# The order of work in the second step of a two-step graph layer, changed in four of seven parts

## The chip, the core and the metric

The kernel runs on one core of a Trainium2 chip. The metric is device time in microseconds (us): the median of several executions. A profile is one more execution, recorded by the hardware profiler. Engines are named as in the profile: PE (matrix products and transposes), DVE (vector), ACT (scalar functions), POOL (GpSimd, which also issues the indirect gathers) and SP (which issues the other transfers). PEld is PE's loading of weights, which overlaps its products.

## The reference

The input is x (3327 x 256) and a sparse weighted adjacency matrix adj (3327 x 3327, about four entries in a row beside the diagonal). After a layer norm and a relu, two steps of the same kind follow, and a last layer norm is added to x:

```python
R = S + jnp.eye(N, dtype=X.dtype)
R = R / R.sum(-1, keepdims=True)
for n in range(STEPS):                       # 2
    A = _top_p_attention(Xa, W1, W2, W3)     # softmax(q k^T), cut to the top 0.9 of its mass, row sums 1
    Xf = R @ Xf
    Xa = A @ Xa
    Z = Z + Xf @ U1[n].T + Xa @ U2[n].T
h = X + Z
```

The costly part is A: 3327 logits in each of 3327 rows, their exponentials, the smallest set of the largest ones that holds 0.9 of each row's sum, and the product of what is left with Xa.

## The kernel before

**Tiles.** A row tile is 128 rows of the matrix ("row i" below is such a tile), and there are 26. One row of exponentials is a tile e of 128 x 3328 in SBUF; it stays there while its threshold is found and is cut in place.

**Two steps, 26 slots each, seven parts in a slot.** The program is written out by Python generators. Each generator is one piece of work on one row, and yields where another may come in between. In slot i of a step, one letter stands for each of them, and the table PLAN (L1001) says in which of the seven parts each is advanced by one stage. The letters of the second step:

- m: `measured_twice` (L635) of row i+1. Its first stage turns the row's sum into a guess (ACT L586 to L591 and L641, POOL L642 to L646). Stage 2 is a pass of ACT over the row (L599, function Relu) and stage 3 a second pass (Sign); stage 4 works out a second guess (DVE L653 and L654, ACT L655 to L657, POOL L658 to L660), stage 5 is a third pass (Sign), stage 6 works out the exponent of a correction (DVE L665 and L666, ACT L668 to L671, POOL L673 to L678).
- n: the rest of m of the slot before, for row i. Its stage 7 is one ACT instruction (L680) that reads what POOL's L678 wrote; stage 8 is DVE L682 to L685 and gives the threshold's guess.
- d: `settle` (L693) of row i, all on DVE: a pass over the row that copies what lies below the guess (L699), twice ten MAX8 (L704), then six rounds of MAX8 and MATCH_REPLACE8 (L711, L713) in two stages, which give the exact threshold (L718 to L723).
- c: the rest of d of the slot before: the pass over the row that cuts it at the threshold (DVE L726), then L727 to L730.
- w: `weights` (L551) of row i+2: one stage is one of four pieces of logits, two products on PE (L566) into a PSUM buffer of two banks (pool ps_l, two buffers) and an exponential on ACT (L570; the last piece L574 and L576).
- q: the first two stages of `weights` of row i+3, which are those of `project` (L517): first the products for queries and law (PE L525, L527) and their copies to SBUF (ACT L530 and L534), then DVE L540 on the copy mq and six POOL instructions on ms (L543 to L548).
- s: `spread` of row i (PE L868, then DVE L984), the sparse product with R. g: `refetch` of row i+2 (five indirect gathers on POOL, L860). f: `finish` of row i-2 (DVE L891, L459, L460; POOL L466, L467; DVE L898; POOL L899 to L901; the transfer out).

Around the letters, each part begins with four transposes of a row on PE (L771) and their copy on ACT (L773), two parts ahead of use, and ends with a piece of the row sum: four products of 128 x 256 (L785) that add up in the one buffer pa. A row's sum starts in part 5 of the slot in which the row is cut and ends in part 4 of the next slot; there ACT scales it into SBUF (L792), and then the next row's sum may start in pa.

**What sets the order.** PE, ACT and DVE run in the order in which the text writes the instructions: at the end, every instruction of these three is tied to the one before it on its engine (L1067 to L1070). POOL and SP are not tied; their order is chosen when the program is built, by when inputs are ready in the builder's own estimate, and is fixed from then on. Waits between engines are on semaphores.

The loop over the parts:

```python
for k in range(PARTS):
    ...
    if summing:
        sums.turn(g, min(i, NT - 1))
    for c in "bb" + PLAN[step][k]:
        next(work[c], None)
    if summing:
        ended = sums.sum(g)
```

Of the kernel before, what the change touches and what calls it, by code (L numbers as in the profile page):

```python
# [342 lines left out]
def guess_graph_layer(ctx, tc, x, adj, w1t, w2t, w3t, u1t, u2t, ln_g, ln_b, out, flag):  # L343
# [646 lines left out]
    def refetch(t):  # L990
# [8 lines left out]


    PLAN = (("mdsssa", "mdsssa", "edawwp", "sda", "mpdea", "mdgawwq", "emdgq"),  # L1001
            ("cmss", "cnms", "wwnfd", "mdsss", "smwqdfg", "mqdfg", "mwdf"))
    LATE = (1, 4)
    trace, begin = nc.cur_bb.bb.instructions, len(nc.cur_bb.bb.instructions)
    work = dict(m=none, d=none, f=none)
# [71 lines left out]
@with_exitstack  # L1077
def tile_graph_layer(ctx, tc, *args):
    keep = ctx.enter_context(tc.tile_pool(name="keep", bufs=1))
    flag = keep.tile([1, 1], I32, tag="flag", name="flag")  # L1080
    guess_graph_layer(tc, *args, flag)
    failed = tc.nc.values_load(flag[0:1, 0:1], min_val=0, max_val=1 << 20)
    with tc.If(failed > 0):
        search_graph_layer(tc, *args)
# [34 lines left out]
```

## Time and profile before

| what | value |
|---|---|
| median of 3 runs | 1568.15 us (1564.48 to 1574.11) |
| the profiled execution, its own time | 1572.46 us |
| its span, first to last instruction | 1570.7 us |
| granted TensorE clock, mean | 0.944 |
| second step, from its first pieces to the end | about 899 to 1571 us of the span |
| row sums' copies (L792) of the second step | first at 980.24, last at 1552.69 |
| between two of them, most rows | 23.53 to 23.56 us |
| two longer slots | 25.48 and 24.59 us |
| the last four | 20.60, 22.01, 19.54 and 13.59 us |

How to read the lines that follow. A line of a timeline has the start in us from the span's start, the duration, the engine, the line of the kernel, the operation, what it writes and reads with shapes, and in square brackets the idle time of that engine just before it and what released it. An idle time is shown only where it is over a few tenths. In a view by windows, each engine has its busy time and in brackets its count of instructions. A stalled instruction counts as busy: POOL's time includes what it stands still for.

### The profile page before, as it was taken

To read this page: it belongs to the slowest core of one execution; us is meant where nothing else is said; L and a number is where in the kernel's file an instruction comes from. 1 tells how busy PE (TensorE), PEld (TensorE's weight loads), DVE (VectorE), ACT (ScalarE), POOL (GpSimd) and SP (SyncE) were. 2 spreads that over 40 slices of the span, in tenths; PEclk is the share of its full clock that TensorE was granted. 3 is DMA by queue.
4 is the path that set the end of the run, shared out by engine and by line. 5 is a ranking of instruction groups with operands and counts; after the bars stand their busy time and mean duration, and the time that the engine had idled before them with its cause. 6 is when DMAs were issued, how large, how long until landed. Compare 5 with 4: busy or idle time off the path is not lost.

```text
span 1570.7 us, 22630 instructions
## 1 busy us (share of the span) xinstructions
PE 1331.4 (85%) x6495; PEld 997.6 (64%) x6495; DVE 1227.8 (78%) x3824; ACT 1104.2 (70%) x2476; POOL 1004.7 (64%) x1491
## 2 busy tenths in 40 slices
PE   5857888988988989889898937998998999899884
PEld 3523666766666767667676725776776767767674
DVE  4457788878987878787786248989988889889892
ACT  5527566757766677677674378898898898898941
POOL 6313464564755656655565156888888888888842
PEclk9978998999999999999999968999999999999997
DMA  7554343443533543444423121122122122122200
GB/s 218 167 163 128 107 128 103 117 129 104 142 114 99 150 111 113 137 115 111 125 63 89 58 72 51 56 77 71 56 76 67 55 81 63 58 81 64 58 18 20
DMA packets 97687, 149.81 MB, mean 95 GB/s; under 512 B 15985, under 2 KB 60528, under 8 KB 97552
## 3 DMA queue, kind: packets, MB, share of 16 engines
q1 hardware_dynamic: 78400, 104.00, 21.7%
q0 software_dynamic: 16640, 42.69, 10.7%
q10 hardware_dynamic: 2512, 1.57, 0.3%
q8 instruction: 54, 0.88, 0.2%
q14 instruction: 81, 0.66, 0.2%
HBM read 120.93 MB, written 27.28 MB: 94 GB/s over the span
## 4 chain that ended last, share of the span: by engine, by line
PE 35%; POOL 22%; ACT 19%; DVE 10%; issue 7%; DMA 4%; another core or an unknown queue 1%; SPq 0%; ACTq 0%; POOLq 0%; DVEq 0%
PE pa L785 17%; ACT ja L599 9%; POOL xg L860 7%; PE pt L771 5%; POOL g L677 4%; PE pr L868 4%; PE pl L566 4%; DMA at<-in_adj 3%; ACT e L570 3%; ACT eT L773 2%; PE pz L881 2%; DVE e L726 2%; DVE cand L704 1%; POOL rstd L467 1%; DVE fm L803 1%
## 5 line engine op out<-in xcount | busy, mean ns | idle before, releaser
L773 ACT COPY eT<-pt 128x512 f32<-128x512 f32 (+1 forms) x364 | 201.3, 554 | 238.4 <-PE pt L771 168.4
L785 PE MATMUL pa<-xw,eT 128*128 128x256 f32 x1352 | 334.9, 390 | 29.3 <-ACT xa L792 28.5
L785 PE MATMUL pa<-x,eT 128*128 128x256 f32 x1352 | 351.4, 404 | 4.1 <-ACT eT L773 2.4
L851 POOL DMA_INDIRECT ac<-in_adj,index x130 | 179.8, 1383 | 247.0 <-DVE mq L540 160.7
L599 ACT ACTIVATE ja<-e,g 128x3328 uint8<-128x3328 f32 x106 | 325.7, 3073 | 0.1
L785 PEld LDWEIGHTS pa<-xw,eT 128*128 128x128 f32 x1352 | 252.6, 193 | 93.0 <-ACT xa L792 33.7
L785 PEld LDWEIGHTS pa<-x,eT 128*128 128x128 f32 x1352 | 261.3, 201 | 58.7 <-issue 16.3
L704 DVE MAX8 cand<-w 128x8 f32<-128x168 f32 (+1 forms) x1040 | 251.3, 317 | 0.0
L771 PE MATMUL pt<-ident,e 128*128 128x128 f32 x1144 | 181.8, 280 | 38.7 <-DVE e L726 35.4
L771 PEld LDWEIGHTS pt<-ident,e 128*128 128x128 f32 x1144 | 145.0, 145 | 77.7 <-issue 32.3
L860 POOL DMA_INDIRECT xg<-bx,index x130 | 163.2, 1255 | 48.2 <-issue 34.9
L566 PE MATMUL pl<-k,qT 64*128 64x416 f32 x832 | 187.8, 556 | 4.7 <-ACT qT L530 4.2
L699 DVE SCALAR_TENSOR_TENSOR w<-e,g 128x3328 f32<-128x3328 f32 x44 | 163.9, 3725 | 0.7
L860 POOL DMA_INDIRECT xg<-vx,index x130 | 134.0, 1031 | 43.9 <-issue 35.0
L726 DVE SCALAR_TENSOR_TENSOR e<-e,rec 128x3328 f32<-128x3328 f32 x44 | 162.0, 3681 | 0.1
L868 PE MATMUL pr<-xg,ac 128*128 128x257 f32 (+1 forms) x520 | 137.7, 387 | 23.4 <-DVE s L984 20.0
L803 DVE TENSOR_REDUCE fm<-at 128x4 f32<-128x512 f32 (+1 forms) x182 | 115.8, 638 | 52.1 <-DMA at<-in_adj 50.4
L570 ACT ACTIVATE e<-pl 128x832 f32<-128x832 f32 x132 | 113.2, 866 | 7.6 <-PE pl L566 6.8
L868 PEld LDWEIGHTS pr<-xg,ac 128*128 128x128 f32 x520 | 90.0, 193 | 33.9 <-DVE s L984 20.3
L566 PEld LDWEIGHTS pl<-k,qT 64*128 64x128 f32 x832 | 71.4, 190 | 51.3 <-issue 42.7
L711 DVE MAX8 bb<-cand 128x8 f32<-128x160 f32 x286 | 92.7, 324 | 6.4
L884 DVE TENSOR_TENSOR sv<-pz,x 128x256 f32<-128x256 f32 x26 | 11.0, 423 | 97.3 <-ACT xw L882 89.9
(221 smaller groups left out, 2211.6 us busy)
## 6 DMA issues: line engine op xcount, KB each, us to landing
at<-in_adj SPq DMA_DIRECT2D x156, 256.0 KB
cx<-ac SPq DMA_DIRECT2D x26, 384.0 KB
ac<-cx SPq DMA_DIRECT2D x26, 384.0 KB
bx<-e SPq DMA_DIRECT2D x26, 128.5 KB
own<-bx SPq DMA_DIRECT2D x26, 128.5 KB
x<-in_x SPq DMA_DIRECT2D x13, 256.0 KB
xr<-in_x SPq DMA_DIRECT2D x26, 128.0 KB
ax<-e SPq DMA_DIRECT2D x26, 128.0 KB
```

What stands on the lines that cost most here:

```text
L566: PE.matmul(pl[:, a, :wd], qT[p, :], keys[step][p].rearrange("p a b -> p (a b)")[:, c : c + wd], start=True, stop=True)
L570: S.activation(e.rearrange("p (a n) -> p a n", a=2)[:, :, c : c + wd], pl[:, :, :wd], AF.Exp, accum_out=za[:, n : n + 1])
L599: S.activation(ja, e, f, bias=guess, scale=sign, accum_out=total)
L699: V.scalar_tensor_tensor(w, e, col(16), e, ALU.is_lt, ALU.mult, accum_out=d2)
L704: V.max(cand[:, 8 * s : 8 * s + 8], w[:, s * SEG : min(NP, (s + 1) * SEG)])
L726: V.scalar_tensor_tensor(e, e, at(1), e, ALU.is_ge, ALU.mult, accum_out=ra)
L771: PE.transpose(pt[:, j, :], e[:, (j0 + j) * P : (j0 + j + 1) * P], ident)
L773: S.copy(eT[:, :w, :], pt[:, :w, :])
L785: PE.matmul(self.pa, eT[:, c - 4 * k, :], self.xa[:, j, :], start=c == 0, stop=c == NT - 1)
L851: G.indirect_dma_start(out=ac[:, k, :], out_offset=None, in_=rows, in_offset=bass.IndirectOffsetOnAxis(ap=index[:, t, k : k + 1], axis=0), ...
L860: G.indirect_dma_start(out=xg[:, k, :w], out_offset=None, in_=rows, in_offset=bass.IndirectOffsetOnAxis(ap=index[:, t, k : k + 1], axis=0))
L868: PE.matmul(pr[:, :w], ac[:, k, :], own if k == KT - 1 else xg[:, k, :w], start=k == 0, stop=k == KT - 1)
```

## The change

One line of the table PLAN, that of the second step, is written anew. The first step, the stages themselves and all other code stay.

```diff
     PLAN = (("mdsssa", "mdsssa", "edawwp", "sda", "mpdea", "mdgawwq", "emdgq"),
-            ("cmss", "cnms", "wwnfd", "mdsss", "smwqdfg", "mqdfg", "mwdf"))
+            ("cmss", "cnms", "nmfd", "dwwsss", "smdfg", "mqdfgwwq", "mdf"))
     LATE = (1, 4)
```

Read part by part, in the second step:

- Part 3: the two pieces of logits (ww) leave its start. The second ACT pass over a row (m, stage 3) comes here from part 4, behind n and ahead of f and d.
- Part 4: the first two pieces of logits come here, behind d and ahead of the last three s. m is gone.
- Part 5: the third piece of logits (w) and the first stage of the projection (q) leave it.
- Part 6: the order is now m (the third ACT pass), q (first stage), d, f, g, two pieces of logits (third and fourth), q (second stage, with DVE L540 and POOL L543 to L548). Before, it was m, q (second stage), d, f, g.
- Part 7: the fourth piece of logits leaves it.

In each slot the same stages run for the same rows as before: m still advances six times, w four times, q twice.

## Prediction

> **What bounds the kernel now.** I read the page first, then the timelines of the second step (from 899 us on), one engine at a time, then the chain of waits there. The diff leaves the first step alone, so only the second counts. The page shows four busy engines and no plain bound:
>
> ```profile
> PE 1331.4 (85%) x6495; PEld 997.6 (64%) x6495; DVE 1227.8 (78%) x3824; ACT 1104.2 (70%) x2476; POOL 1004.7 (64%) x1491
> ```
>
> In the second step the row sum's copy (L792) returns every 23.53 to 23.56 us for most rows: that is the slot. One such slot in the view by windows (busy us by engine, PE, PEld, DVE, ACT, POOL):
>
> ```profile
> 1158.90:1182.50 23.60, 21.42 (x113) 16.58 (x111) 21.22 (x67) 20.82 (x43) 20.70 (x31) 1.00 0.22 68
> ```
>
> All four have 20.7 us or more, so the end is set by how they hand over. POOL's timeline in this slot, start and duration first:
>
> ```profile
> 1177.52 0.57 POOL L676 TENSOR_TENSOR g<-g,half 128x1 f32<-128x1 f32 x1
> 1178.19 3.82 POOL L677 TENSOR_SCALAR g<-g 128x1 f32<-128x1 f32 x1
> 1182.12 0.31 POOL L678 TENSOR_SCALAR g<-g 128x1 f32<-128x1 f32 x1
> ...
> 1183.89 3.56 POOL L643 TENSOR_SCALAR g<-g 128x1 f32<-128x1 f32 x1
> ```
>
> L677 and L643 work on 128x1 and take 0.30 and 0.19 us in other slots. They stand still under DVE's two passes over a row:
>
> ```profile
> 1171.78 0.21 DVE L540 SCALAR_TENSOR_TENSOR mq<-mq 128x64 f32<-128x64 f32 x1
> ...
> 1174.63 0.27 DVE L665 TENSOR_SCALAR g<-oa,g 128x1 f32<-128x1 f32 x1 [0.30 <-ACT ja L599]
> ...
> 1178.25 3.68 DVE L726 SCALAR_TENSOR_TENSOR x<-x,rec 128x3328 f32<-128x3328 f32 x1
> ```
>
> POOL's queue has no wait for another engine in this slot: 23.54 us = 16.63 of its own (20.70 less the two stalls, plus gaps of about 0.1 between instructions and 0.3 between gathers) + stalls of 3.52 and 3.37. ACT does wait, for POOL:
>
> ```profile
> 1158.92 0.29 ACT L680 ACTIVATE g<-g 128x1 f32<-128x1 f32 x1 [2.18 <-POOL g L678]
> ...
> 1167.86 0.48 ACT L792 ACTIVATE xa<-pa,ra 128x256 f32<-128x256 f32 x1
> ...
> 1170.70 0.28 ACT L534 COPY mq<-pq 128x130 f32<-128x130 f32 x1
> 1170.86 0.60 ACT L773 COPY eT<-pt 128x512 f32<-128x512 f32 x1
> 1171.34 3.09 ACT L599 ACTIVATE ja<-x,g 128x3328 uint8<-128x3328 f32 x1
> ```
>
> From here on times count from the start of L680 (1158.92). The loop that closes a slot: L680 0; L792 8.94; third ACT pass 12.42 to 15.46; L665 15.71; L726 19.33 to 23.01; L677 released; L678; next L680 23.54.
>
> [...] here two gathers under these passes took 4.22 and 4.40 us where 0.95 is usual, at 944.99 and 949.71. So neither kind of POOL work hides under a pass. [...] the pass behind L680 needs nothing from POOL and waits 2.18 us with it.
>
> **The change part by part.** No instruction is added or removed; four things move within a slot.
>
> 1. *The second ACT pass to the third part, the first two logits pieces behind it.* On ACT the order from 0 is pass, copy, two pieces (1.69), copy, pass (3.08), L792. It becomes pass, copy, pass, copy, two pieces, L792. The same five things stand ahead of L792: it starts at 8.94 again. That no 3 us pass stands directly before it buys nothing, since ACT has no gap there. PE reaches the row sum's end about 1.6 us earlier (its logits come later) but the next row's sum needs the single pa buffer: its wait for L792 grows from 1.31 to about 3 us. On DVE, L653's wait of 1.22 for the second pass goes: the pass now ends at 6.8, DVE is there at 7.9. DVE is 1.2 ahead until part 6. Value on the closing loop: nothing, because L655 still queues behind L792 and the copy (9.76).
>
> 2. *Third piece and projection leave part 5.* On ACT 0.85 + 0.30 us less lie between L657 and the copy eT ahead of the third pass. But that copy waits for PE: L792 ends 9.42, the sum's eight instructions 1.83, transposes 0.60, so 11.9; in the kernel before it started at 11.94. The third pass stays at 12.42. Value: nothing; ACT idles 1.1 us there instead.
>
> 3. *Projection copies (L530, L534) behind the third pass.* Now L534 is done at 15.46 + 0.15 + 0.28 = 15.89. L540 on DVE needs it, and the written order puts L540 after the rounds of the sixth part and *before* L665. DVE is there at 14.1 (the rounds ended at 15.4 before; less the 1.22 of part 1 and L540's own place) and waits 1.8. L540 at 15.92, L665 at 16.16 where it was 15.71: **+0.45**. Queued behind: L666, the last three rounds, L898, L726 (19.33 -> 19.78). POOL's six instructions on ms (L543 to L548, 2.30 us from L543's start to L673's) also wait for L540: they began at 15.08, straight after L467, and now begin at 16.24 (L540 + 0.32, as at 938.66 and 938.98).
>
> 4. *What is late next.* POOL then has ms 2.30 and L673 to L678: 18.54, 19.03, 19.42, 19.76 for L676. DVE's L726 starts at 19.78. An instruction that starts 0.06 to 0.08 before a pass is stalled too (L677 above, L673 at 1201.83). So L676 is caught rather than L677. The pass ends at 23.46; L676 needs 0.4 more (a 0.73 us L900 ended 0.5 after such a pass), L677 and L678 0.8: 24.65, L680 at once. The new slot is 24.65, **+1.11** = 0.45 for L726 and 0.66 for one more instruction behind it. If L676 slips through, L726 waits 0.6 and L677 is caught: 24.55. POOL no longer fills its queue: it has 1.1 us idle before L543, inside a longer slot.
>
> The moved pieces (third and fourth, now behind L534 on ACT; L668 at 18.05 instead of 16.26) are covered: ACT would reach the next L680 at 22.2 and waits for POOL until 24.65. Without that cover the 1.1 us of part 2 would count. PE is done with its slot at 23.2 and has its wait for L792 as reserve. Gathers on POOL (five of 1.25) keep their place; SP's queue gets no new wait.
>
> Sum, against the profiled execution's own 1572.5 (span 1570.7 plus 1.8 around it). 21 slots have the loop whole: 21 x 1.11 = +23.3. At the step's start L678 ended before L726 began, at 944.34 and 968.05, and L680 followed within 1 to 2.5 us; with L540 late both are caught. The next L680s move from 944.96 and 970.39 to about 949.4 and 975.5: +5. One gather waited 2.1 us at 1189, and that slot and the next were 3.0 longer in all; POOL's new slack takes some 2 of it: -2. The first slot puts ten gathers ahead of L660 (L665 waits 8.24): a different order on POOL there could give 0 to 4, taken as -1. The last four rows have no projection, and L653 waits for nothing in them: 0. Sum **+25**: 1597 on that execution's scale, which is 4.3 above the median of the runs shown; on the median **1593**.
>
> **Unknown costs.** POOL's order is not the written one (L466 and L467 stand ahead of L543 though written after), so the new one is not certain: ms first is what its readiness asks for, since L540 precedes L665 on DVE. Interleaved, L678 is still last of twelve. Per slot: 0.7 (L677 caught) to 1.4 (L675 caught), so +12 to +32 with the start between 0 and +6.
>
> **Rivals.**
> - *POOL stays the bound, no change.* If L673 to L678 run ahead of the ms group, L678 ends at 16.5 + 2.6 = 19.1, before L726; then the closing loop is short and POOL's 16.63 + 6.9 sets the slot: 23.54, 1564 to 1574. For it: POOL never waits today. Against: L673 becomes ready 0.5 us after L543.
> - *Faster.* DVE's lost waits (1.22 + 0.30) come through and the slot falls to 22.7, the shortest at the step's start: 21 x 0.84 = -18, 1550. This needs L678 done before L726 *and* POOL's passes overlapping idle time; it decides at a POOL demand under 22.7, and POOL's own 16.63 + 6.9 is 23.5 wherever a pass falls. Nearly excluded.
> - *Worse.* Gathers come to stand behind L658 and L659 (ready 10.9), so that ms and all of L673 to L678 fall under the pass: L678 near 26, 21 x 2 = +42, 1610. Against: the gathers' buffer is free at 5.3, long before.
>
> **How the numbers follow.** Loop over L540: 0.72, own range 1578 to 1604. No change 0.15. Worse 0.09. Faster 0.04. About 1% (15.7 us) is what a measurement of this kernel can tell from no change. Slower by more: 0.72 less 0.04 for its low end, plus 0.09 = 0.77. Within: 0.15 + 0.04 = 0.19. Faster 0.04. The range takes in most of the no-change case and the bounds of the stall: 1570 to 1606.
>
> **What would show it.** Right: slots of 24.3 to 25 in the second step; DVE waiting 1.5 to 2 us at L540 for L534; POOL waiting about 1 us at L543 for L540; L676 or L677 at 3.5 us or more; PE's wait for L792 near 3; no wait at L653. Wrong: L673 ahead of L543 on POOL, slots of 23.5, or a third pass that starts before 12.

## The result, and the profile after

The changed kernel takes 1644.37 us (median of 4 runs, 1640.33 to 1645.67), the kernel before 1567.33 on the same chip: 1.048 of it, interval 1.044 to 1.052. The prediction was 1593, with a range of 1570 to 1606. It had the sign, and 25 of the 77 us.

The profiled execution of the new kernel took 1640.33 us, 67.9 more than that of before. (The medians are 77 apart, as the one profiled before was 5 us above its median and the one after 4 below.) From the copies L792 in ACT's timeline, the 67.9 come together as follows:

| where | before | after | difference |
|---|---|---|---|
| first L792 of the second step, from the span's start | 980.24 | 985.21 | +5.0 |
| the 21 slots after it | 496.71 (mean 23.65) | 559.11 (mean 26.62) | +62.4 |
| from there to the end of the span | 93.8 | 94.3 | +0.5 |

In the first part of the page, after, only PE has more work to show, though it executes the same 6495 instructions:

```profile
PE 1366.5 (83%) x6495; PEld 1029.9 (63%) x6495; DVE 1227.8 (75%) x3824; ACT 1104.9 (67%) x2476; POOL 1006.9 (61%) x1491
```

They took 35.1 us longer. The new slots run from 24.96 to 27.17 us. The view by windows, after, for one of the shortest and one of the longest (slot, busy time of PE, PEld, DVE, ACT and POOL, granted clock, DMA share, GB/s):

```profile
1027.70:1052.66 24.96, 21.15 (x112) 16.70 (x111) 21.11 (x64) 20.80 (x42) 20.92 (x31) 1.00 0.22 64
1293.22:1320.39 27.17, 23.64 (x112) 18.76 (x111) 21.11 (x65) 20.80 (x43) 20.89 (x31) 0.87 0.20 59
```

DVE, ACT and POOL have the same work in both. PE's 112 instructions take 2.49 us more in the second, and its mean granted clock there is 0.87. PE's timeline, after, shows which instructions: the eight products that start a row sum, once L792 has emptied pa.

```profile
1037.17 1.99 PE L785 MATMUL pa<-xw,eT 128*128 128x256 f32 x8 [3.71 <-ACT xa L792]
...
1302.69 3.78 PE L785 MATMUL pa<-xw,eT 128*128 128x256 f32 x8 [3.53 <-ACT xa L792]
...
1309.83 1.99 PE L785 MATMUL pa<-xw,eT 128*128 128x256 f32 x8
```

The wait for L792 was 1.3 us; now it is over 3. In two of the 21 slots the eight products behind it still take 1.99 us, in nine 2.67 to 3.45, and in ten 3.78, about half their rate. A few us later (1309.83) they are at full rate again. What is late next is in ACT's timeline, after, in the same slot; times from L680 (1293.22) are 8.94 for L792, 14.14 for the copy eT and 14.62 for the third pass, which was at 12.42:

```profile
1293.22 0.29 ACT L680 ACTIVATE g<-g 128x1 f32<-128x1 f32 x1 [2.70 <-POOL g L678]
...
1302.16 0.48 ACT L792 ACTIVATE xa<-pa,ra 128x256 f32<-128x256 f32 x1
...
1307.36 0.59 ACT L773 COPY eT<-pt 128x512 f32<-128x512 f32 x1 [3.25 <-issue]
1307.84 3.07 ACT L599 ACTIVATE ja<-e,g 128x3328 uint8<-128x3328 f32 x1
```

ACT's 3.25 us are called "issue", but the copy follows the products and transposes on PE (the transposes L771 start at 1306.26 and take 1.06, so they end at 1307.32); in the 24.96 us slot the same wait is 1.04 us and is put down to PE's L771. DVE's timeline, after:

```profile
1311.36 0.23 DVE L540 SCALAR_TENSOR_TENSOR mq<-mq 128x64 f32<-128x64 f32 x1 [4.22 <-ACT mq L534]
...
1311.52 0.27 DVE L665 TENSOR_SCALAR g<-oa,g 128x1 f32<-128x1 f32 x1
1315.13 3.68 DVE L726 SCALAR_TENSOR_TENSOR e<-e,rec 128x3328 f32<-128x3328 f32 x1
```

And POOL's, after:

```profile
1311.71 0.34 POOL L543 TENSOR_SCALAR ms<-mq,ms 128x1 f32<-128x1 f32 x1 [3.49 <-DVE mq L540]
...
1314.93 3.92 POOL L675 TENSOR_SCALAR g<-g 128x1 f32<-128x1 f32 x1
...
1320.05 0.31 POOL L678 TENSOR_SCALAR g<-g 128x1 f32<-128x1 f32 x1
```

L726 catches L675, so that three instructions (L676 to L678) follow the pass where one did; then L680 starts the next slot. The table of waits, after, for 1275 to 1492 us puts the same chain together (us in total, times, longest):

```profile
PE pa L785 <- ACT xa L792: 31.6, 9, 3.7
DVE mq L540 <- ACT mq L534: 31.4, 8, 4.2
POOL ms L543 <- DVE mq L540: 25.4, 8, 3.5
ACT g L680 <- POOL g L678: 21.3, 8, 2.7
```

In the kernel before (1155 to 1395 us) the first of these was 13.3 us in 9 waits, and the wait of ACT for L678 was the same 21.3, in 9.

The slot with the full clock, 24.96 us (two of the 21 are so), is what the prediction's working should be held against. There L540 starts at 15.94 after L680 (predicted 15.92), L543 at 16.29 (16.24), L726 at 19.71 (19.78). So the 62.4 us split, with no experiment yet, into 21 x (24.96 - 23.65) = 27.5 for the predicted loop and 21 x (26.62 - 24.96) = 34.9 for PE's clock. The second is close to the 35.1 us that PE's busy time grew by.

### The profile page after: what moved, and what is told of

The parts are those of the page before. It is cut to its first block, busy times and chain, and to the rows that moved or that the text cites. A ratio compares the mean times of both kernels' runs of the same rounds, so it can differ in the third digit from the quotient of the medians.

```text
span 1638.6 us, 22607 instructions
## 1 busy us (share of the span) xinstructions
PE 1366.5 (83%) x6495; PEld 1029.9 (63%) x6495; DVE 1227.8 (75%) x3824; ACT 1104.9 (67%) x2476; POOL 1006.9 (61%) x1491
## 4 chain that ended last, share of the span: by engine, by line
PE 34%; ACT 31%; POOL 14%; DVE 7%; issue 7%; DMA 4%; another core or an unknown queue 2%; SPq 0%; ACTq 0%; POOLq 0%; DVEq 0%
ACT ja L599 16%; PE pa L785 16%; POOL g L675 5%; PE pt L771 4%; PE pr L868 4%; ACT eT L773 4%; DMA at<-in_adj 3%; PE pl L566 3%; ACT e L570 3%; PE pz L881 3%; POOL g L676 1%; PE pz L930 1%; PE pk L486 1%; ACT e L574 1%
## 5 line engine op out<-in xcount | busy, mean ns | idle before, releaser
L785 PE MATMUL pa<-xw,eT 128*128 128x256 f32 x1352 | 359.7, 412 | 78.7 <-ACT xa L792 78.5
L785 PEld LDWEIGHTS pa<-xw,eT 128*128 128x128 f32 x1352 | 268.1, 205 | 135.1 <-ACT xa L792 84.6
L771 PE MATMUL pt<-ident,e 128*128 128x128 f32 x1144 | 186.9, 286 | 26.9 <-DVE e L726 12.3
L566 PE MATMUL pl<-k,qT 64*128 64x416 f32 x832 | 192.1, 553 | 5.9 <-ACT qT L530 5.4
L771 PEld LDWEIGHTS pt<-ident,e 128*128 128x128 f32 x1144 | 150.2, 148 | 65.7 <-issue 18.2
L860 POOL DMA_INDIRECT xg<-bx,index x130 | 157.7, 1213 | 51.3 <-issue 33.2
L699 DVE SCALAR_TENSOR_TENSOR w<-e,g 128x3328 f32<-128x3328 f32 x44 | 164.3, 3733 | 0.7
L726 DVE SCALAR_TENSOR_TENSOR e<-e,rec 128x3328 f32<-128x3328 f32 x44 | 162.1, 3683 | 0.1
L868 PE MATMUL pr<-xg,ac 128*128 128x257 f32 (+1 forms) x520 | 141.7, 395 | 23.2 <-DVE s L984 20.2
L570 ACT ACTIVATE e<-pl 128x832 f32<-128x832 f32 x132 | 114.0, 872 | 8.4 <-PE pl L566 6.5
L566 PEld LDWEIGHTS pl<-k,qT 64*128 64x128 f32 x832 | 85.5, 198 | 49.2 <-issue 36.9
L675 POOL TENSOR_SCALAR g<-g 128x1 f32<-128x1 f32 x26 | 83.7, 3218 | 2.5
```

The lines of the kernel that those rows point to most:

```text
L566: PE.matmul(pl[:, a, :wd], qT[p, :], keys[step][p].rearrange("p a b -> p (a b)")[:, c : c + wd], start=True, stop=True)
L570: S.activation(e.rearrange("p (a n) -> p a n", a=2)[:, :, c : c + wd], pl[:, :, :wd], AF.Exp, accum_out=za[:, n : n + 1])
L675: G.tensor_scalar(col(12), col(12), col(12), 1.0e-12, ALU.mult, ALU.add)
L699: V.scalar_tensor_tensor(w, e, col(16), e, ALU.is_lt, ALU.mult, accum_out=d2)
L771: PE.transpose(pt[:, j, :], e[:, (j0 + j) * P : (j0 + j + 1) * P], ident)
L785: PE.matmul(self.pa, eT[:, c - 4 * k, :], self.xa[:, j, :], start=c == 0, stop=c == NT - 1)
```

## The experiments

Two theories at the start. **Clock:** the longer idle time costs PE its full rate, and the rest is the predicted loop over L540 and POOL. **Order:** POOL's and DVE's order alone makes the longer slot, and PE's longer products hide behind it.

The kernels ran on several chips, on which the kernel before took 1580.02 us (experiments 1 to 4), 1492.16 (8 to 11), 1494.37 (5, 6 and 12) and 1491.87 (7). They differ in the clock granted in the first step: from 300 to 700 us it was 0.95 to 0.97 in the kernel before, and 1.00 in experiment 10. So each ratio is against the kernel before on the same chip; the changed kernel itself ran on the first chip alone. "Slot" is the mean of 21 slots of the second step from L792 to L792 in the one profiled execution (23.65 before, 26.62 after), and a slot's "sum" is the eight products behind the L792 that opens it.

**1. The projection back in part 5, only the second pass moved (third and fourth pieces stay behind f and g).**

```diff
-            ("cmss", "cnms", "nmfd", "dwwsss", "smdfg", "mqdfgwwq", "mdf"))
+            ("cmss", "cnms", "nmfd", "dwwsss", "smqdfg", "mqdfgww", "mdf"))
```

> The changed kernel with only the projection put back: its first stage in part 5 and its second in part 6, both ahead of the rounds, as before the change; the logits stay in two pairs and the second pass in part 3. Theory A (late L540 delays L665 and POOL's ms group, and PE's long wait for L792 sends its clock down): L540 waits for nothing, POOL's ms group follows L467 at once, slots of 23.5 us where PE's first eight products after L792 take 2.0 us, and up to 24.4 where they take 3.8 (then ACT's 21.1 us of work and 3.3 us of idle time make the slot): 1566 to 1592 us. Theory B (the second pass in part 3, or the new order of the gathers on POOL, is what costs): the projection makes little difference, over 1615 us.

Measured: 1.0058 (1.0035 to 1.0081), slot 24.10. Slots of 24.6 to 25.3 us (26.6 once) and of 23.3 to 24.1 take turns, but for four in a row of 23.5. PE's timeline of this kernel, and then POOL's, a short slot (from 1080.76) and a long one (from 1104.26):

```profile
1081.30 3.54 PE L785 MATMUL pa<-xw,eT 128*128 128x256 f32 x8 [1.35 <-ACT xa L792]
...
1104.80 1.99 PE L785 MATMUL pa<-xw,eT 128*128 128x256 f32 x8 [0.31 <-ACT xa L792]
```

```profile
1092.12 0.33 POOL L678 TENSOR_SCALAR g<-g 128x1 f32<-128x1 f32 x1
...
1114.58 3.87 POOL L674 TENSOR_SCALAR g<-g 128x1 f32<-128x1 f32 x1
```

In the short slot the slow sum makes L665 and L726 late; L726 (1092.83) finds L678 done, and ACT's L680 waits for nothing. In the long one the sum is fast, L726 (1114.68) catches L674, and L680 waits 3.05 us for L678. PE is then idle at the slot's end, for 2.01 us ahead of the two short projection products and for 1.35 behind them, and the next sum is slow again (3.46). So the clock can be lost even where short work splits the idle time. It isn't a rule: after 1.69 and 1.35 us a sum once took 3.78 and once 2.00, and after 0.60 and 1.35 us three took 1.99 and one 3.62.

**2. Only the projection moved.**

```diff
-            ("cmss", "cnms", "wwnfd", "mdsss", "smwqdfg", "mqdfg", "mwdf"))
+            ("cmss", "cnms", "wwnfd", "mdsss", "smwdfg", "mqdfgq", "mwdf"))
```

> The kernel before with only the projection moved, first stage behind the third pass and second stage behind the rounds; logits and second pass stay where they were. Theory A: L540 waits for L534, ms and L673 to L678 fall under L726, slots of 24.6 to 25.0 while PE's clock holds and towards 27 where it does not (PE has the piece of logits in part 5, so its wait for L792 is 2 to 2.6 us[...]): 1592 to 1640 us. Theory B: at most 1575 us.

Measured: 1.0311 (1.0257 to 1.0366), slot 25.80. PE's timeline of this kernel:

```profile
1430.62 1.99 PE L785 MATMUL pa<-xw,eT 128*128 128x256 f32 x8 [2.81 <-ACT xa L792]
1455.58 3.41 PE L785 MATMUL pa<-xw,eT 128*128 128x256 f32 x8 [2.81 <-ACT xa L792]
1482.22 2.76 PE L785 MATMUL pa<-xw,eT 128*128 128x256 f32 x8 [2.81 <-ACT xa L792]
1508.36 1.99 PE L785 MATMUL pa<-xw,eT 128*128 128x256 f32 x8 [2.81 <-ACT xa L792]
```

The idle time is the same in all, and the eight take 1.99, 2.76 or 3.41 us. The slot that starts with a sum of 1.99 us has 24.96 (1430.62 to 1455.58, and L675 is caught in it), the two behind it 26.6 and 26.1. So this part of the change alone has both costs.

**3. Only the second pass and the first two pieces moved.**

```diff
-            ("cmss", "cnms", "wwnfd", "mdsss", "smwqdfg", "mqdfg", "mwdf"))
+            ("cmss", "cnms", "nmfd", "dwwsss", "smwqdfg", "mqdfg", "mwdf"))
```

> The kernel before with only the second pass moved to part 3 and the first pair of logits behind it in part 4; third and fourth piece and the projection stay. Theory A: the wait at L653 goes, PE's wait for L792 stays near 1.3 us, POOL's order and waits stay, slots of 23.5 us: 1562 to 1573 us. Theory B: 1585 us or more.

Measured: 1.0076 (1.0032 to 1.0119), slot 24.23. The expected value was missed, by another wait than the one looked for. PE's timeline of this kernel:

```profile
1275.81 1.06 PE L566 MATMUL pl<-k,qT 64*128 64x416 f32 x4 [2.50 <-ACT x L570]
1277.65 3.12 PE L785 MATMUL pa<-xw,eT 128*128 128x256 f32 x8
```

The first two pieces stand now right ahead of the third, both buffers ps_l are full until ACT's L570 has read one, and PE waits 2.5 us for it with the sum's products queued behind: a third place for an idle time, and again a long sum. Where this wait is 2.5 us or more, six of seven sums take 2.69 to 3.78 us; where it is 1.05 to 1.46, none of seven does. As in experiment 1, the long sums (here in the second half of the step) stand in every second slot, and the slot behind such a one is long (25.5).

**4. The changed kernel, with PE kept occupied.** Part 2 of a slot makes its four transposes (row part k = 2) seven times, with the same values.

```diff
-                for j in range(w):
+                for j in list(range(w)) * (7 if self.step and k == 2 else 1):
```

> The changed kernel, with the four transposes of the row's third part in the second step made seven times (the same values into the same buffer, in PE's wait for L792), so that PE is busy 2.7 us longer there and idle under 1 us. The result is unchanged. Theory A: PE's clock holds, the sum behind L792 takes 2.0 us and not 3.8, the transposes of the next part come 2 us sooner, slots of about 24.9 us as the two short ones at the start had: 1598 to 1610 us. Rival C (the slow products follow from the longer slot and set nothing): 1640 to 1650 us.

Measured: 1.0200 (1.0143 to 1.0257) where the changed kernel itself has 1.048; slot 24.76, ten of the 21 from 24.67 to 24.71. *More* work on PE made the kernel faster. PE's timeline of this kernel, and then POOL's:

```profile
1270.14 1.99 PE L785 MATMUL pa<-xw,eT 128*128 128x256 f32 x8 [0.78 <-ACT xa L792]
```

```profile
1280.12 0.43 POOL L675 TENSOR_SCALAR g<-g 128x1 f32<-128x1 f32 x1
1280.64 3.89 POOL L676 TENSOR_TENSOR g<-g,half 128x1 f32<-128x1 f32 x1
```

All sums take 1.99 us, and what is left is the loop of the prediction: in 16 of the 21 slots L676 is caught, and most of these are 24.7 us long; in the other five L677 is caught. The order theory has no place for this, so it is out.

**5. The same with three instead of seven.**

```diff
+                for j in list(range(w)) * (3 if self.step and k == 2 else 1):
```

> The changed kernel with these transposes made three times, 0.9 us of work in PE's wait: idle time before the sum about 2.6 to 2.9 us (3.3 to 3.7 without, 0.8 with seven). If the products are slow whenever PE was idle for long enough, with a length at which it turns, slots alternate as with the projection alone (2.81 us idle, about every second sum slow): 25.3 to 26.2 us on average, 1.028 to 1.040 of before. If only the length of the wait counts and not a turn: about 26 us in every slot alike.

Measured: 1.0317 (1.0289 to 1.0344), slot 25.76. The idle time is 2.4 to 2.85 us (3.28 once), and 12 of the 21 sums take 2.4 us or more: a dose between none and seven, an effect between. None of the six sums after less than 2.75 us is long.

**6 and 7. Experiment 1 with PE kept occupied**, seven times and four times, to see whether the second pass in part 3 costs anything else.

```diff
             ("cmss", "cnms", "nmfd", "dwwsss", "smqdfg", "mqdfgww", "mdf"))
...
+                for j in list(range(w)) * (7 if self.step and k == 2 else 1):
```

> The changed kernel with the projection put back ahead of the rounds (as in the run with the projection back) and the transposes of the row's third part made seven times, so that PE's clock holds. Theory A: neither term is left, POOL's queue sets the slot: 23.5 to 23.7 us from one row sum's copy to the next (the run without the repeats had 24.10 on average, with one slot in two slow), 0.997 to 1.008 of before. If the second pass in part 3 has a cost of its own: over 23.9 us.

Measured: 1.0064 (1.0039 to 1.0088), slot 24.06 (within 0.02 of it in 16 of the 21), no long sum. Inconclusive: with the repeats PE has 23.9 us of work in such a slot and is itself full. With four (`* (4 if ...)`); the order is that of experiment 1 here too, so the third piece of logits stands in part 6, not where it was before:

> The order with only the second pass moved and the third piece and projection where they were before, with the transposes of row part 2 made four times (the same values again), so that TensorE is kept occupied but is not full: about 21.3 + 1.35 = 22.7 us of work in a slot. Theory A (the clock of TensorE alone makes the alternation of about 25.0 and 23.4 us): no slow sums (8 products in 1.99 us), slots of 23.5 to 23.7 us, 0.998 to 1.004 of the kernel before. Theory B (the second pass in part 3 has a cost of its own): sums at 1.99 us and slots still above 23.9 us.

Measured: 0.9998 (0.9986 to 1.0011), slot 23.64. PE's timeline of this kernel:

```profile
1262.00 1.99 PE L785 MATMUL pa<-xw,eT 128*128 128x256 f32 x8 [0.71 <-ACT xa L792]
```

All slots but three are the 23.5 us of before, with L677 and L643 caught as in the kernel before. So what experiment 1 moves, the second pass and the pieces of logits, costs only the clock, and is worth nothing else: the prediction's value for it, but only while PE keeps its rate.

**8 and 9. The ms group behind L678 on POOL**, so that the pass stalls work that nobody waits for: in the changed kernel q's second stage goes behind m in part 7, and L543 is tied behind L678.

```diff
-            ("cmss", "cnms", "nmfd", "dwwsss", "smdfg", "mqdfgwwq", "mdf"))
+            ("cmss", "cnms", "nmfd", "dwwsss", "smdfg", "mqdfgww", "mqdf"))
...
+            tc.add_manual_dep(one_, last.name, IN_ORDER, reason="ms behind the exponent")
```

> The changed kernel with the projection's second stage moved behind m in part 7, so that L540 stands behind L665 and L666 on DVE, and POOL's ms group tied behind L678. PE's long idle time before the sum stays. Theory A (three terms: L540 ahead of L665, the pass on L673 to L678, and PE's clock): the first two are gone, the last stays; L678 is done before L726, and ACT's 21.1 us of work with 3.3 us of idle time before the third pass make the slot: 24.2 to 24.6 us where the products are slow, 1.010 to 1.016 of before. If the order on POOL and DVE did not matter: 26.5 to 27.2 us, 1.045 or more.

Measured: 1.0162 (1.0145 to 1.0179), slot 24.67, between 22 and 27.5 (29.7 once). This is near the expected number, but not in the expected way. L543 and L547 now take the stalls (3.72 and 3.52 us), and ACT's L680 no longer waits for POOL. But PE's idle time before the sum is gone as well (0.13 us in most slots), and all 21 sums take 1.99 us: the term of the clock that was to make these slots isn't there. The table of waits of this kernel, for 1196 to 1392 us, shows others in its place:

```profile
DVE g L665 <- POOL g L658: 21.7, 7, 3.6
PE pt L771 <- DVE e L726: 16.2, 6, 3.9
```

Which of them makes a slot of 24.67 us isn't shown. With the transposes seven times as well:

> The same, and the transposes of the row's third part made seven times so that PE's clock holds (the same values into the same buffer). Theory A: all three terms gone, POOL's queue is full again, slots of 23.5 to 23.7 us, 0.997 to 1.005 of before. A remaining cost of the second pass in part 3 or of the order of the gathers would show as slots over 23.9 us, 1.007 or more.

Measured: 1.0213 (1.0196 to 1.0230), slot 24.89, where 23.5 was expected. POOL's timeline of this kernel:

```profile
1247.06 3.99 POOL L901 TENSOR_TENSOR s<-s,xr 128x256 f32<-128x256 f32 x1
...
1253.72 0.73 POOL L899 TENSOR_TENSOR xr<-xr,bet 128x256 f32<-128x256 f32 x1 [1.30 <-DMA xr<-in_x]
```

The ms group went ahead of L900 and L901 on POOL, and here DVE's other pass (L699) catches L901. The buffer xr comes free late, its next transfer lands late, and L899, which waited for nothing in the kernel before, waits 1.3 us for it; the gathers behind L899 and with them L658 are late, and DVE's L665 waits 2.8 to 3.4 us for L658 in most slots. In experiment 8, where L547 is caught and not L901, L899 and L665 wait as long (1.2 to 1.5 and 2.9 to 3.2 us in most slots). The repeats nearly fill PE here too (23.5 us of work in slots of 24.6). A stall taken off one instruction of a full queue was given to another.

**10 to 12. The kernel before, with less work on POOL.** L901, then L900 and L901, go to DVE in the last stage of `finish`; then, with both, L543 is tied behind L678 of the same slot.

```diff
-        G.tensor_tensor(y, y, gam, ALU.mult)
-        G.tensor_tensor(y, y, xr, ALU.add)
...
+        V.tensor_tensor(y, y, gam, ALU.mult)
+        V.tensor_tensor(y, y, xr, ALU.add)
```

> The kernel before with L901 (the residual's add, 0.73 us on POOL) made by DVE in the last stage of finish. If POOL's queue sets the slot of the kernel before, the slot falls by 0.8 to 22.7 us: 21 x 0.8 = 17 us less, 0.988 to 0.992. If DVE or ACT sets it, no less than 0.997.

> The kernel before with L900 and L901 both made by DVE in the last stage of finish, 1.5 us off POOL and 0.8 more on DVE. POOL as the bound: slots of 22.0 to 22.7 us (DVE has 22.0 then), 0.980 to 0.990. DVE or ACT as the bound: 0.995 or more.

> The kernel before with L900 and L901 on DVE and POOL's ms group tied behind L678 of the same slot; the projection stays where it was. L678 is done before L726 in every slot, so the next L680 does not wait for the pass; what is left is ACT's 21.1 us and POOL's 15.1 + 6.9: slots of 22.3 to 22.8 us in place of 22.4 and 23.5 in turn, 0.978 to 0.986 of before. If it is 23.2 or more, L680's wait was not what lengthened every second slot.

Measured: 0.9957 (0.9943 to 0.9971), 0.9913 (0.9896 to 0.9929) and 0.9866 (0.9839 to 0.9892); slots 23.12, 23.24 and 22.47. (The profiled execution of the second was its slowest, 1486.08 us with a median of 1478.59, so its slot may be too long.) The first two gain less than POOL alone as the bound was to give, and more than DVE or ACT as the bound. The third has the expected slot, and its time is at the edge of what was expected. It is faster than both kernels. POOL's timeline of it:

```profile
1276.58 0.33 POOL L678 TENSOR_SCALAR g<-g 128x1 f32<-128x1 f32 x1
1276.91 0.34 POOL L543 TENSOR_SCALAR ms<-mq,ms 128x1 f32<-128x1 f32 x1
...
1277.89 3.24 POOL L546 TENSOR_SCALAR ms<-ms,mq 128x1 f32<-128x1 f32 x1
```

L678 is done before L726 (1277.31), the stall falls on L546, and ACT's L680 waits for POOL in one of the 21 slots only. PE's sums keep 1.99 us with an idle time of 0.16: in such a slot of 22.43 us PE has 21.35 of work and DVE 21.33, so these two come next.

## Why the prediction was wrong

**What failed is one clause of part 1**: PE's "wait for L792 grows from 1.31 to about 3 us", left without a price, and in part 4 the same wait called a "reserve". The wait was foreseen to within 0.7 us (3.25 to 3.71 measured). What it does to the work behind it was not: in part 2's sum "the sum's eight instructions 1.83, transposes 0.60, so 11.9", the 1.83 (from the first product to the first transpose) became 3.57 in the slot shown, the 0.60 became 1.06, and the copy eT came at 14.14. PE's idle time was no reserve here, as PE's rate behind it fell. The term that was put at nothing measured 34.9 us by the slots of the changed kernel, and 39 (21 x (26.62 - 24.76)) by experiment 4, where L676 is caught in place of L675.

**The clue was in the trace of before.** PE's timeline of the kernel before, two sums:

```profile
1191.92 1.99 PE L785 MATMUL pa<-xw,eT 128*128 128x256 f32 x8 [1.31 <-ACT xa L792]
...
1217.41 3.78 PE L785 MATMUL pa<-xw,eT 128*128 128x256 f32 x8 [2.71 <-ACT xa L792]
```

The second opens the second of the two longer slots, which the prediction put down to a gather alone. The first of them (25.48, 1.94 above the usual 23.54) comes before this sum and is the gather's; it left PE idle for 2.71 us, the sum took 1.79 us longer, and the second slot (24.58) is 1.04 above the usual. So at most about a third of their 3.0 us is the clock's, but this one line showed what a wait of about 3 us could do in each slot.

What the traces show of this loss is its size, half the rate (3.78 us against 1.99), and the full rate a few us later (1.99 at 1309.83, 7.1 after the start of the sum of 3.78). They show no length of idle time at which it sets in: after 2.81 us of idle time in experiment 2, 11 of 19 sums were long; 1.69 + 1.35 us with short products between cost the rate once and once not; and in the changed kernel 3.40 and 3.71 us each failed once to cost it.

**Part 3 was right.** L540 at 15.94 and L726 at 19.71 in slots at full clock; no wait at L653 any more; L543 ahead of L673 on POOL. **Part 4 was right in mechanism, and small in size**: L676 was to be caught and L675 was, as it started at 19.52 (19.42 in the prediction's sums) and L726 at 19.71 (19.78), 0.19 us later, so the slot is 24.96 instead of 24.65. With PE kept occupied L675 starts 0.30 us ahead and slips through, and the slot is 24.67. The prediction had this as its upper bound (+1.4). **The start** was +5.0, as predicted and in the predicted way: the two L680s came at 949.55 and 976.27 (about 949.4 and 975.5 in the prediction), each behind an L678 that came late because DVE's pass had caught L676. The first slot gave nothing (L680 at 928.67, 928.75 before) where -1 was taken. The tail was 0.5 instead of 0. The gather's -2 is inside the 27.5: 21 x (24.96 - 23.54) is 29.8, less the 2.4 by which the longer slots of before had raised its mean. Loop, start and tail thus make 33 where the prediction had 25, and the clock made up the other 35.

**The rivals.** "POOL stays the bound" asked for L673 ahead of L543; it isn't. "Faster" asked for L678 done before L726; L675 is caught. "Worse" asked for gathers so late that ms and L673 to L678 all fall under the pass. Two of the five gathers did come between L660 and L658, but at no cost: POOL finishes L658 to L467 behind them and still waits for L540 (1.27 us in the 24.96 us slot). No rival had PE in it, and the range ended at 1606.

**What stays open**: what decides which sum is long after the same idle time; what sets the slot in experiment 8; and what the 1.1 us are by which experiment 12's slot exceeds PE's 21.35 us of work. The parts are not additive: all but the projection +0.6% (experiment 1), the projection alone +3.1%, together +4.8%. Both lengthen PE's idle time before the same sum, which would explain it, but no run shows that this is all of it.

## What to carry to other kernels

An engine's wait is a reserve only if its rate doesn't depend on it: before PE's wait of 1 us is let grow to 3, look in the trace for the same products behind a long and a short idle time (here 3.78 us behind 2.71, and 1.99 behind 1.31), and price the difference on whatever follows. Where a pass of DVE stalls POOL (here L677 took 3.82 us in place of 0.30), don't ask how long the stall is, but which instruction it falls on and who waits for that one. To tell a clock from an order, give PE more work in its idle time, but not so much that it is full (experiment 6): if the kernel gets faster with it, as here (1.020 of before where it was 1.048), order alone doesn't explain the time.

## What was not expected of the hardware

- The same eight products after the same 2.81 us of idle time took 1.99, 2.76 or 3.41 us. Repeating four transposes seven times (about 2.7 us more of PE's work in each slot, an estimate from the wait of 3.25 to 3.71 us that became 0.78) took 1.9 us off the slot (26.62 to 24.76, on different chips).
- A POOL instruction of about 0.3 us that started 0.19 us before DVE's pass was held for the whole pass (3.92, the changed kernel); one that started 0.30 us before took 0.43 (experiment 4). The prediction had reckoned with 0.06 to 0.08.
